# Adjacency loads paced by the projection loop, adj @ x spread into the mixing, and sums scattered to natural order

## The chip, the cores and the metric

The kernel runs on one core of one Trainium2 chip. The metric is device microseconds (us) of one execution; a lower number is better. A profile is one execution, so its span can lie a few us from the median.

Engine names in profile lines: PE is TensorE (PEld its weight loads), DVE is VectorE, ACT is ScalarE, POOL is GpSimd, SP is SyncE, which here only issues transfers. L540 is line 540 of that kernel's own file; the same statement has another line number in another kernel.

## The reference

Four graph layers act on `x` of 8 x 2048 x 64, each followed by a residual and a layer norm. The change touches only the first layer and the way its result is handed on.

```python
# layer 0: hypergraph attention
h = x @ W                                               # the loop over h
s = leaky_relu(h @ a_node, 0.2)
alpha = softmax(where(H.T > 0, s, NEG)); agg = alpha @ h
beta = sigmoid((h @ a_gn)[:, None] + (agg @ a_ge)[..., None])
all_he = elu(beta * h + (1 - beta) * agg)
se = attn_scores(elu(agg))                              # tanh(f @ fcW + fcb) @ av
g = sum_e softmax(where(H > 0, se, NEG)) * all_he       # the slot loop
industry = (adj / deg) @ (x @ W_ind)                    # adj @ x, "filler" matmuls
out = weighted_pair(industry, g)                        # the mixing
x = layernorm(x + out)
# layer 1
x = layernorm(x + (dinv * (adj + I) * dinv) @ x @ W.T)
# layers 2 and 3: unchanged by this edit
```

A node belongs to few hyperedges, so `g` is computed by slots: nodes are sorted by how many hyperedges they have, 128 nodes to a tile, and tile t needs only as many slots as its fullest node. There are 57 slots in 16 tiles. `adj` is 2048 x 2048 float32, held as 16 tiles of 1 MB.

## The kernel before

Its first 640 us run in stages on all engines. The loop over h has 16 steps; it projects `x`, stores the rows `hs` in HBM for later gathering, and accumulates the hyperedge sums `pagg`. The table chain turns `pagg` into small tables, while the first filler matmuls (`du`, row sums of `adj`) run in between. `fill(n)` issues the next n matmuls of adj @ x; there are 64 of `du` and 512 of `ug`, about 0.23 us each.

```python
XT = NT // 8; XB = XT * NP                       # 8 x buffers; 14 adjacency tiles issued at once
for t in range(NT - XT):
    if t in (0, 1):
        tc.keep_in_program_order(nc.gpsimd.tensor_copy(seen_x, xt[2 * t + 1][:, 0, 0:1]))
    load_adj(t)                                  # 1 MB, from GpSimd's queue
# ...
for t in range(NT):                              # the loop over h
    # ph = xt[t] @ bd66 (4 matmuls)
    fetch_xt(t + XB)
    st = pa.tile([P, HROW], F32, tag="st", name="st", bufs=4)
    # seen, exponentials, st, ex on DVE and ACT
    nc.scalar.dma_start(hs_hbm[t * P:(t + 1) * P, :], st)
    # pagg += m_n.T @ ex
# ... table chain with fill(24), fill(14), fill(14), fill(12)
```

A one-hot is a matrix of zeros with a single 1 for each node; multiplied with a table it picks, for every node of a tile, the row of the node's hyperedge in that slot. `pz` is that row plus the node's own row, `ps` the same for the few columns of scores, from which the factors `R` and `co` are made. In the slot loop each slot has three `pz` matmuls, nine filler matmuls, three DVE operations, one exponential and one GpSimd sum:

```python
for t in range(NT):
    S, both, ohs, R, co = now                    # begin(t): gathered rows, hi/lo split, ps, coefficients
    for s in range(S):
        # pz = rows + one_hot[s] @ table (3 matmuls)
        if s == 0 and t + 1 < NT:
            fill(3)
            now = begin(t + 1)
        fill(9)
        if s == max(0, S - 5) and t + 2 < NT:
            slots(t + 2, pps, "mm", 3)           # GpSimd makes the one-hots of tile t + 2
        nc.vector.tensor_tensor(z, z, R[:, s, :, None].to_broadcast([P, B, F]), ALU.mult)
        y = pl.tile([P, B, F], F32, tag="y", name="y", bufs=2)
        nc.scalar.activation(y, z, AF.Exp, bias=-1.0)
        nc.vector.scalar_tensor_tensor(y, z, 1.0, y, op0=ALU.max, op1=ALU.min)
        # y * co on DVE; acc + y on GpSimd (not for s == 0)
    nc.sync.dma_start(gs_hbm[t * P:(t + 1) * P, :], acc.rearrange("p b f -> p (b f)"))   # sorted order
for _ in filler:
    pass
```

The mixing has 16 steps; each gathers its rows of `g` back to natural order. From the sixth step on, layer 1's matmuls are the filler (10 in each of four places a step). Layer 1 leaves three of its four results in SBUF; the third goes through HBM.

```python
    for j in range(JT):                          # mix_parts(i): 4 indirect gathers a step
        nc.gpsimd.indirect_dma_start(out=gn[:, j, :], in_=g_rows, in_offset=IndirectOffsetOnAxis(rank4[...]), ...)
# ...
for i in range(steps + 1):
    k = 10 if i > NCH else 0                     # no filler in the first five steps
    # mix_parts, fill(k), mix_weigh, fill(k), mix_scores, fill(k), mix_end, fill(k)
fill(40)
nc.scalar.dma_start(xn[2], x2_hbm[:])
```

## Time and profile before

The median was 2234.11 us in 3 runs (2231.68 to 2234.51).

| stage (profile of before) | from, to (us) | length | what fills it |
|---|---|---|---|
| loop over h | 21.0, 80.4 | 59.4 | DMA until 60 us, then steps of 1.85 us |
| table chain | 80.4, 110.1 | 29.7 | filler, waits for GpSimd |
| slot loop | 110.1, 288.5 | 178.4 | PE 94% busy |
| mixing alone | 288.5, 347.0 | 58.5 | PE 41.5 busy |
| mixing and layer 1 | 347.0, 639.6 | 292.6 | PE 82% busy |
| layers 2 and 3 | 639.6, 2233.5 | 1593.9 | not changed |

### The profile page before, as it was taken

How to read it: one execution, taken by the hardware profiler on the slowest of the kernel's cores; microseconds unless marked ns; L12 is line 12 of the kernel's file. 1: busy time of each engine (PE TensorE's matmuls, PEld its weight loads, DVE VectorE, ACT ScalarE, POOL GpSimd, SP SyncE). 2: the span in 40 equal slices, each digit the busy share in tenths (PEclk: the TensorE clock that was granted, in tenths of full speed). 3: DMA queues.
4: the chain of work that ended last, by engine and by line, in shares of the span. 5: the costliest groups of instructions: out<-in, count | busy, mean ns of one | idle time of the engine just before them, and what ended most of it. 6: DMA issues, size and time to landing. Idle time of an engine off the chain costs nothing. (4 is left out here: it accounts for less than half of the span.)

```text
span 2233.5 us, 19741 instructions
## 1 busy us (share of the span) xinstructions
PE 1979.0 (89%) x7292; PEld 1279.6 (57%) x7292; DVE 1115.8 (50%) x1833; ACT 374.7 (17%) x688; POOL 553.8 (25%) x507
## 2 busy tenths in 40 slices
PE   4899969888749999799999999999896999999994
PEld 3578725555634444474465456456444777777773
DVE  4478846666532222217845864772883233333322
ACT  1223333232111111010010010001001112222110
POOL 2377866564222322100100010110110010110102
PEclk7899979999869999899999999999998999999997
DMA  9412333222210000100000000000001112111110
GB/s 368 162 54 93 106 103 95 90 66 71 81 16 0 19 19 19 43 1 7 7 5 5 7 8 3 7 10 0 10 5 41 38 27 55 37 52 38 48 29 21
DMA packets 65706, 104.31 MB, mean 47 GB/s; under 512 B 27312, under 2 KB 27344, under 8 KB 63360
## 3 DMA queue, kind: packets, MB, share of 16 engines
q1 hardware_dynamic: 54432, 70.51, 10.4%
q0 software_dynamic: 5856, 25.89, 3.5%
q10 hardware_dynamic: 5312, 6.56, 0.9%
q8 instruction: 59, 0.97, 0.2%
q14 instruction: 47, 0.39, 0.1%
HBM read 76.13 MB, written 26.80 MB: 46 GB/s over the span
## 5 line engine op out<-in xcount | busy, mean ns | idle before, releaser
L1020 PE MATMUL py<-wp,xg 128*128 128x512 f32 x1024 | 448.6, 597 | 8.5 <-DVE fcav L1025 5.8
L1020 PEld LDWEIGHTS py<-wp,xg 128*128 128x128 f32 x1024 | 193.6, 191 | 254.4 <-issue 216.2
L177 PE MATMUL u<-adj,hi 128*128 128x512 f32 x768 | 258.0, 417 | 0.0
L177 PE MATMUL u<-adj,lo 128*128 128x512 f32 x768 | 249.0, 404 | 0.0
L967 PE MATMUL u<-pt,xn 128*128 128x512 f32 x512 | 230.5, 609 | 8.3 <-DVE u L976 7.1
L1025 DVE TENSOR_TENSOR fcav<-py,emb_n 128x512 f32<-128x512 f32 x256 | 177.1, 692 | 52.1 <-PE py L1020 37.2
L1028 POOL TENSOR_TENSOR r<-r,bias 128x256 f32<-128x256 f32 x32 | 23.3, 729 | 636.2 <-DVE r L1026 636.2
L1026 DVE TENSOR_REDUCE r<-fcav 128x32 f32<-128x512 f32 x256 | 175.4, 685 | 8.1
L967 PEld LDWEIGHTS u<-pt,xn 128*128 128x128 f32 x512 | 98.5, 195 | 132.0 <-issue 117.0
L645 PE MATMUL u<-adj,vh 128*128 128x512 f32 x512 | 158.8, 409 | 14.7 <-ACT vh L168 10.9
L177 PEld LDWEIGHTS u<-adj,hi 128*128 128x128 f32 x768 | 144.3, 192 | 41.2 <-issue 11.2
L177 PEld LDWEIGHTS u<-adj,lo 128*128 128x128 f32 x768 | 146.1, 192 | 34.3
L645 PE MATMUL u<-adj,vl 128*128 128x512 f32 x512 | 152.1, 399 | 0.0
L156 POOL TENSOR_TENSOR ln_r<-ln_e,neg_half 128x8 f32<-128x8 f32 x64 | 106.1, 1659 | 169.3 <-DVE ln_e L154 167.9
L961 DVE TENSOR_SCALAR pt<-pt 128x512 f32<-128x512 f32 x64 | 48.8, 781 | 175.4 <-ACT pt L960 174.0
L1116 DVE SCALAR_TENSOR_TENSOR fcav<-fcav,ar 128x512 f32<-128x512 f32 x64 | 44.3, 693 | 176.4 <-ACT ar L1115 176.3
L1098 POOL TENSOR_TENSOR r<-r,xn 128x512 f32<-128x512 f32 x16 | 20.4, 1278 | 435.0 <-DVE r L1097 435.0
L645 PEld LDWEIGHTS u<-adj,vh 128*128 128x128 f32 x512 | 96.4, 190 | 45.1 <-ACT vh L168 12.4
L965 POOL TENSOR_TENSOR acc<-acc,pt 128x512 f32<-128x512 f32 x60 | 79.6, 1327 | 165.9 <-DVE pt L961 163.1
L645 PEld LDWEIGHTS u<-adj,vl 128*128 128x128 f32 x512 | 96.6, 189 | 22.2 <-issue 0.7
L150 ACT ACTIVATE r<-ln_c 128x512 f32<-128x512 f32 x64 | 40.4, 631 | 264.7 <-DVE ln_c L146 253.3
L762 POOL DMA_INDIRECT gn<-gs_hbm,rank x64 | 69.7, 1089 | 34.2 <-PE pg L180 14.6
(339 smaller groups left out, 2748.5 us busy)
## 6 DMA issues: line engine op xcount, KB each, us to landing
adj<-in_adj_t POOLq DMA_DIRECT2D x16, 1024.0 KB
fcav<-in_adj_t SPq DMA_DIRECT2D x64, 256.0 KB
x_hbm<-r SPq DMA_DIRECT2D x20, 256.0 KB
hs_hbm<-st ACTq DMA_DIRECT2D x16, 292.0 KB
xt<-in_x_t SPq DMA_DIRECT2D x16, 256.0 KB
xc<-in_x_n SPq DMA_DIRECT2D x16, 256.0 KB
u_hbm<-ut SPq DMA_DIRECT2D x16, 256.0 KB
gs_hbm<-acc SPq DMA_DIRECT2D x16, 256.0 KB
```

Source lines behind the costliest of these rows:

```text
L150: nc.scalar.activation(r, xc, AF.Square)
L156: nc.gpsimd.tensor_tensor(rstd, vare, neg_half[:, :groups], ALU.pow)
L177: tc.keep_in_program_order(nc.tensor.matmul(*args, **kw))
L645: nc.tensor.matmul(u[c], lhsT=half[:, j, :], rhs=adj[t][:, cols(c)], start=t == 0 and i == 0, stop=ends and not own,)
L762: nc.gpsimd.indirect_dma_start(out=gn[:, j, :], out_offset=None, in_=g_rows, in_offset=bass.IndirectOffsetOnAxis(ap=rank4[:, p, c * JT + j ...
L961: nc.vector.tensor_scalar(pt, pt, 1.0, None, op0=ALU.max)
L965: nc.gpsimd.tensor_tensor(acc, acc, pt, ALU.add)
L967: nc.tensor.matmul(u[p], lhsT=xn[p][:, t, :], rhs=pt, start=t == 0, stop=t == NT - 1)
L1020: nc.tensor.matmul(py.rearrange("p o d -> p (o d)"), lhsT=xg[b][:, q, cols(j, P)], rhs=wp[:, q, cols(k)], start=q == 0, stop=q == 1,)
L1025: nc.vector.tensor_tensor(pr, py, e_b, ALU.mult)
L1026: nc.vector.tensor_reduce(r[:, j, b, cols(k, OH)], pr, AX.X, ALU.add)
L1116: nc.vector.scalar_tensor_tensor(a, a, 1.0, ar.bitcast(F32), op0=ALU.mult, op1=ALU.not_equal, accum_out=left[:, t, k:k + 1],)
```

## The change

Four ideas belong together. The adjacency loads no longer go out at once but after certain steps of the loop over h, so that the row writes need not queue behind them. Filler leaves the slot loop (9 to 6 a slot) for the mixing's first five steps, where TensorE was idle. The sums of the slot loop are scattered to natural order, so that 64 gathers of the mixing become 16 plain loads. The pools are laid out anew for this: fewer x buffers, `x` chunks fetched in the loop, and all of layer 1's results but the last through HBM. The diff, cut to its core:

```diff
-    XT = NT // 8
-    XB = XT * NP
+    XT, XB = 1, NP
@@ adjacency
-        for t in range(NT - XT):
-            if t in (0, 1):
-                tc.keep_in_program_order(nc.gpsimd.tensor_copy(seen_x, xt[2 * t + 1][:, 0, 0:1]))
+        def load_adj_after(t, what):
+            tc.keep_in_program_order(nc.gpsimd.tensor_copy(seen_x, what))
             load_adj(t)
+        for t in range(5):
+            load_adj_after(t, xt[min(t, 3)][:, 0, 0:1])
+        paced = {1: 5, 2: 6, 4: 7, 5: 8, 7: 9, 8: 10, 10: 11, 11: 12, 13: 13, 14: 14}
@@ loop over h
+            if t in paced:
+                load_adj_after(paced[t], seen[:, t, 0, 0:1])
+            if t in (NT // 2, NT // 2 + 2):
+                c = (t - NT // 2) // 2
+                fetch(0, c)
+                parts(0, c)
@@ one-hots
-            made = nc.gpsimd.tensor_scalar(o, slot, float(s + 1), None, op0=ALU.is_equal)
+            eng = nc.vector if t == 0 and s % 3 < 2 else nc.gpsimd
+            made = eng.tensor_scalar(o, slot, float(s + 1), None, op0=ALU.is_equal)
@@ table chain: fills 24 + 14 + 14 + 12 become 24 + 14 + 10 + 24, tile 0's one-hots come after them in program order
@@ slot loop
-                fill(9)
+                fill(6)
-            nc.sync.dma_start(gs_hbm[t * P:(t + 1) * P, :], acc.rearrange("p b f -> p (b f)"))
-        for _ in filler:
-            pass
+            nc.gpsimd.indirect_dma_start(
+                out=gs_hbm[:], out_offset=bass.IndirectOffsetOnAxis(ap=order[:, t:t + 1], axis=0),
+                in_=acc.rearrange("p b f -> p (b f)"), in_offset=None,
+            )
@@ mixing
-        for j in range(JT):
-            nc.gpsimd.indirect_dma_start(
-                out=gn[:, j, :], out_offset=None, in_=g_rows,
-                in_offset=bass.IndirectOffsetOnAxis(ap=rank4[:, p, c * JT + j:c * JT + j + 1], axis=0),
-            )
+        nc.sync.dma_start(
+            gn, gs_hbm[c * C:(c + 1) * C, p * P:(p + 1) * P].rearrange("(t p) f -> p t f", p=P)
+        )
-        k = 10 if i > NCH else 0
+        k = 10 if i > NCH else 8
@@ layer 1's results
-        if p != 2:
+        if p == NP - 1:
             layernorm(lp, grouped(r), grouped(xn[p][:, wide(c), :]))
         else:
             layernorm(lp, grouped(r), grouped(r))
-            nc.sync.dma_start(x2_hbm[:, wide(c), :], r)
+            nc.sync.dma_start(x2_hbm[p][:, wide(c), :], r)
@@ after the mixing
+    for p in range(2):
+        nc.scalar.dma_start(xn[p], x2_hbm[p][:])
     fill(40)
-    nc.scalar.dma_start(xn[2], x2_hbm[:])
+    nc.scalar.dma_start(xn[2], x2_hbm[2][:])
```

More of the change, by code (lines that the diff above doesn't have):

```diff
@@ L166, in split @@
         lo = pool.tile(shape, F32R, tag=f"{tag}l", name=f"{tag}l", bufs=bufs)
-        steps = (
-            nc.scalar.copy(hi, src),
-            eng.tensor_tensor(lo, src, hi.bitcast(F32) if eng is nc.gpsimd else hi, ALU.subtract),
-        )
-        if pin:
-            for i in steps:
-                tc.keep_in_program_order(i)
+        kept = tc.keep_in_program_order if pin else lambda i: i
+        kept(nc.scalar.copy(hi, src))
+        kept(eng.tensor_tensor(lo, src, hi.bitcast(F32) if eng is nc.gpsimd else hi, ALU.subtract))
         return hi, lo
@@ L198, in tile_gnn_fast @@
     av_col = const.tile([P, 1], F32, name="av_col")
-    rank4 = const.tile([P, NP, NT], U32, name="rank4")
     wrong = const.tile([P, 6], F32, name="wrong")
     nc.vector.memset(wrong, 0.0)
+    va_scope = ExitStack()
+    va = va_scope.enter_context(tc.tile_pool(name="va", bufs=1))
     hy_scope = ExitStack()
@@ L209, in staged @@
     def staged(name):
-        return hy.tile([P, JT, P], F32, tag="x", name=name, bufs=2)
+        return va.tile([P, JT, P], F32, tag="x", name=name, bufs=2)
     def load_adj(t):
@@ L222, in tile_gnn_fast @@
     x1_hbm = [dram.tile([P, NT, P], F32, name=f"x1_hbm{p}") for p in range(NP)]
-    x2_hbm = dram.tile([P, NT, P], F32, name="x2_hbm")
+    x2_hbm = [dram.tile([P, NT, P], F32, name=f"x2_hbm{p}") for p in range(NP - 1)]
     gs_hbm = dram.tile([N, BF], F32, name="gs_hbm")
@@ L253, in slots @@
         for s in range(sum(n > t for n in SLOT_TILES)):
-            o = hy.tile([P, P], F32R, tag="o", name="o", bufs=17)
-            made = nc.gpsimd.tensor_scalar(o, slot, float(s + 1), None, op0=ALU.is_equal)
+            o = hrp.tile([P, P], F32R, tag="o", name="o", bufs=17)
+            eng = nc.vector if t == 0 and s % 3 < 2 else nc.gpsimd
+            made = eng.tensor_scalar(o, slot, float(s + 1), None, op0=ALU.is_equal)
             if t == 0:
@@ L264, in tile_gnn_fast, with fetch, parts @@
     places = {}
-    def products():
-        xc = {}
-        def fetch(p, c):
-            xc[p, c] = staged("xc")
-            load_x(xc[p, c], p, c)
-        part = {}
-        def parts(p, c):
-            part[c] = split(hy, xc.pop((p, c)), f"v{c}", 1, [P, JT, P], nc.gpsimd)
-        for c in range(NCH):
-            fetch(0, c)
-            parts(0, c)
+    xc, part = {}, {}
+    def fetch(p, c):
+        xc[p, c] = staged("xc")
+        load_x(xc[p, c], p, c)
+    def parts(p, c):
+        part[c] = split(va, xc.pop((p, c)), f"v{c}", 1, [P, JT, P], nc.gpsimd, p == 0)
+    def products():
         du = [pph.tile([P, 2, C], F32, tag="ph", name=f"du{g}", bufs=2) for g in range(2)]
@@ L328, in products @@
                             transpose(pt[:, cols(j, P)], deg1[:, k:k + 1].to_broadcast([P, P]))
-                        inv.append(places["sbuf"](f"inv{c}"))
+                        inv.append(va.tile([P, C], F32, name=f"inv{c}"))
                         nc.scalar.copy(inv[c], pt)
                 for c in own:
-                    ut = places["ut"]()
+                    ut = va.tile([P, C], F32, tag="ut", name="ut", bufs=2)
                     nc.vector.tensor_tensor(ut, u[c], inv[c], ALU.mult)
@@ L344, in tile_gnn_fast @@
     pph = ph_scope.enter_context(tc.tile_pool(name="ph", bufs=1, space=PSUM))
-    with tc.tile_pool(name="pa", bufs=1) as pa, tc.tile_pool(name="pa_ps", bufs=1, space=PSUM) as pps:
+    with tc.tile_pool(name="pa_ps", bufs=1, space=PSUM) as pps:
+        pa_scope = ExitStack()
+        pa = pa_scope.enter_context(tc.tile_pool(name="pa", bufs=1))
         xs_scope = ExitStack()
@@ L386, in tile_gnn_fast @@
         nc.gpsimd.memset(avz, 0.0)
-        age = pa.tile([P, F], F32, name="age")
+        age = hy.tile([P, F], F32, name="age")
         nc.gpsimd.dma_start(age, bass.AP(tensor=a_ge.tensor, offset=a_ge.offset, ap=[[0, P], [1, F]]))
@@ L445, in tile_gnn_fast @@
         nc.vector.tensor_reduce(rank, gt, AX.X, ALU.add)
-        for p in range(NP):
-            nc.vector.tensor_scalar(rank4[:, p, :], rank, float(NP), float(p), op0=ALU.mult, op1=ALU.add)
         over = so.tile([P, BINS], F32, name="over")
@@ L504, in tile_gnn_fast @@
         so_scope.close()
-        ta_scope = ExitStack()
         seen = pa.tile([P, NT, B, 2], F32, name="seen")
@@ L533, in tile_gnn_fast @@
             )
-            nc.scalar.activation(ex[:, :, :, F], lr.rearrange("p (k g) -> p k g", k=2), AF.Exp)
+            tc.keep_in_program_order(
+                nc.scalar.activation(ex[:, :, :, F], lr.rearrange("p (k g) -> p k g", k=2), AF.Exp)
+            )
             for k in range(2):
@@ L555, in tile_gnn_fast @@
         adj += [adj_end.tile([P, N], F32R, name=f"adj{t}") for t in range(NT - XT, NT)]
+        load_adj(NT - 1)
         fetch_rows(0)
         fetch_rows(1)
-        for t in range(NT - XT, NT):
-            load_adj(t)
-        ta = ta_scope.enter_context(tc.tile_pool(name="ta", bufs=1))
+        for c in (2, 3):
+            fetch(0, c)
+            parts(0, c)
+        pa_scope.close()
+        hrp_scope = ExitStack()
+        hrp = hrp_scope.enter_context(tc.tile_pool(name="hrp", bufs=1))
+        ta_scope = ExitStack()
+        ta = ta_scope.enter_context(tc.tile_pool(name="ta", bufs=1, side="right"))
         ones_r = ta.tile([P, P], F32R, name="ones_r")
@@ L574, in tile_gnn_fast @@
         nc.vector.reciprocal(den, den)
-        agg = pa.tile([P, G, F], F32, tag="ex", name="agg", bufs=2)
+        agg = ta.tile([P, G, F], F32, name="agg")
         nc.vector.tensor_tensor(agg, gv[:, :, 0:F], den[:, :, None].to_broadcast([P, G, F]), ALU.mult)
-        he = pa.tile([P, G, F], F32, tag="ex", name="he", bufs=2)
+        he = ta.tile([P, G, F], F32, name="he")
         nc.scalar.activation(he, agg, AF.Exp)
@@ L592, in tile_gnn_fast @@
             nc.scalar.activation(tf[:, b], pf, AF.Tanh, bias=fcb_col)
-        fill(14)
-        tab = pa.tile([P, G, F], F32, tag="st", name="tab", bufs=4)
+        fill(10)
+        tab = ta.tile([P, G, F], F32, name="tab")
         tsm = ta.tile([P, 2, G], F32, name="tsm")
@@ L616, in tile_gnn_fast @@
         stack(tab2.rearrange("p (k n) -> p k n", k=2), tab.rearrange("p g f -> p (g f)"), "tabr", False)
-        slots(0, pps, "sm", 2)
-        fill(12)
         pse = pps.tile([P, 2, 2], F32, tag="sm", name="pse", bufs=2)
@@ L631, in tile_gnn_fast @@
         stack(ts2.rearrange("p (i k g) -> p k i g", i=2, k=2), tsm, "tsr", True)
+        slots(0, pps, "sm", 2)
+        fill(NT * NCH - 48 + 8)
         ta_scope.close()
@@ L658, in tile_gnn_fast @@
     with ExitStack() as pb_scope:
-        pb = pb_scope.enter_context(tc.tile_pool(name="pb", bufs=1, side="right"))
         pps = pb_scope.enter_context(tc.tile_pool(name="pb_ps", bufs=1, space=PSUM))
         places["small"] = lambda shape, name: pps.tile(shape, F32, tag="mm", name=name, bufs=3)
-        places["ut"] = lambda: pb.tile([P, C], F32, tag="ut", name="ut", bufs=2)
-        places["sbuf"] = lambda name: pb.tile([P, C], F32, name=name)
         pl = pb_scope.enter_context(tc.tile_pool(name="pl", bufs=1))
@@ L670, in begin @@
             hrow = hrows.pop(t)
-            both = split(hy, hrow[:, 0:BF], "hr", 2, [P, BF], nc.vector if t == 0 else nc.gpsimd, t == 0)
+            both = split(hrp, hrow[:, 0:BF], "hr", 2, [P, BF], nc.vector if t == 0 else nc.gpsimd, t == 0)
             ohs = one_hot.pop(t)
@@ L716, in tile_gnn_fast @@
                     nc.gpsimd.tensor_tensor(acc, acc, y, ALU.add)
-            nc.sync.dma_start(gs_hbm[t * P:(t + 1) * P, :], acc.rearrange("p b f -> p (b f)"))
-        for _ in filler:
-            pass
-    ph_scope.close()
+            nc.gpsimd.indirect_dma_start(
+                out=gs_hbm[:], out_offset=bass.IndirectOffsetOnAxis(ap=order[:, t:t + 1], axis=0),
+                in_=acc.rearrange("p b f -> p (b f)"), in_offset=None,
+            )
+    hrp_scope.close()
     hy_scope.close()
@@ L737, in tick @@
             pending.pop(0)[1]()
-    xn = [None] * NP
-    xn01 = ctx.enter_context(tc.tile_pool(name="xn01", bufs=1))
-    for p in range(2):
-        xn[p] = xn01.tile([P, NT, P], F32, name=f"xn{p}")
-    l1_scope = ExitStack()
-    lp = l1_scope.enter_context(tc.tile_pool(name="l1", bufs=1))
-    lps = l1_scope.enter_context(tc.tile_pool(name="l1_ps", bufs=1, space=PSUM))
     mix_scope = ExitStack()
-    mp = mix_scope.enter_context(tc.tile_pool(name="mix", bufs=1))
-    bd_w1 = on_diagonal(lp, w1_t, "bd_w1")
-    g_rows = gs_hbm[:].rearrange("n (p f) -> (n p) f", f=P)
+    mp = mix_scope.enter_context(tc.tile_pool(name="mix", bufs=1, side="right"))
+    lps_scope = ExitStack()
+    lps = lps_scope.enter_context(tc.tile_pool(name="l1_ps", bufs=1, space=PSUM))
     def wide(c):
@@ L760, in mix_parts @@
         gn = mp.tile([P, JT, P], F32, tag="gn", name="gn", bufs=2)
-        for j in range(JT):
-            nc.gpsimd.indirect_dma_start(
-                out=gn[:, j, :], out_offset=None, in_=g_rows,
-                in_offset=bass.IndirectOffsetOnAxis(ap=rank4[:, p, c * JT + j:c * JT + j + 1], axis=0),
-            )
+        nc.sync.dma_start(
+            gn, gs_hbm[c * C:(c + 1) * C, p * P:(p + 1) * P].rearrange("(t p) f -> p t f", p=P)
+        )
         ut = mp.tile([P, C], F32, tag="ut0", name="ut0", bufs=2)
@@ L804, in mix_end @@
         p, c = divmod(i, NCH)
-        r = lp.tile([P, JT, P], F32, tag="r", name="r", bufs=3)
+        r = mp.tile([P, JT, P], F32, tag="r", name="r", bufs=2)
         load_x(r, p, c)
@@ L810, in mix_end @@
         nc.vector.tensor_tensor(r, pt.rearrange("p (t f) -> p t f", f=P), r, ALU.add)
-        layernorm(lp, grouped(r), grouped(r))
+        layernorm(mp, grouped(r), grouped(r))
         nc.sync.dma_start(x1_hbm[p][:, wide(c), :], r)
-    part = [None] * NCH
     def l1_parts(p, c):
@@ L827, in l1_end @@
         nc.sync.dma_start(x1, x1_hbm[p][:, wide(c), :])
-        r = lp.tile([P, JT, P], F32, tag="r", name="r", bufs=3)
+        r = lp.tile([P, JT, P], F32, tag="r", name="r", bufs=2)
         nc.vector.tensor_tensor(r, po, dinv[:, wide(c), None].to_broadcast([P, JT, P]), ALU.mult)
         nc.gpsimd.tensor_tensor(r, r, x1, ALU.add)
-        if p != 2:
+        if p == NP - 1:
             layernorm(lp, grouped(r), grouped(xn[p][:, wide(c), :]))
@@ L840, in layer1 @@
             own = (2 * g, 2 * g + 1)
-            u = {c: lps.tile([P, C], F32, tag=f"u{c}", name=f"u{c}", bufs=1) for c in own}
+            ug = pph.tile([P, 2, C], F32, tag="ph", name="u1", bufs=2)
+            u = {c: ug[:, c % 2, :] for c in own}
             for t in range(NT):
@@ L871, in all_pairs @@
             yield from layer1(p)
-    filler = all_pairs()
-    def fill(n):
-        for _ in range(n):
-            next(filler, None)
     steps = NP * NCH
     for i in range(steps + 1):
-        k = 10 if i > NCH else 0
+        k = 10 if i > NCH else 8
         if i < steps:
@@ L894, in tile_gnn_fast @@
         if i == NCH:
+            for _ in filler:
+                pass
+            va_scope.close()
+            l1_scope = ExitStack()
+            lp = l1_scope.enter_context(tc.tile_pool(name="l1", bufs=1))
+            bd_w1 = on_diagonal(lp, w1_t, "bd_w1")
             for c in range(NCH):
                 l1_parts(0, c)
+            filler = all_pairs()
     mix_scope.close()
-    xn23 = ctx.enter_context(tc.tile_pool(name="xn23", bufs=1, side="right"))
-    for p in range(2, NP):
-        xn[p] = xn23.tile([P, NT, P], F32, name=f"xn{p}")
+    xnp = ctx.enter_context(tc.tile_pool(name="xnp", bufs=1, side="right"))
+    xn = [xnp.tile([P, NT, P], F32, name=f"xn{p}") for p in range(NP)]
+    for p in range(2):
+        nc.scalar.dma_start(xn[p], x2_hbm[p][:])
     fill(40)
-    nc.scalar.dma_start(xn[2], x2_hbm[:])
+    nc.scalar.dma_start(xn[2], x2_hbm[2][:])
     for _ in filler:
@@ L907, in tile_gnn_fast @@
     l1_scope.close()
+    lps_scope.close()
+    ph_scope.close()
     with tc.tile_pool(name="l2c", bufs=1) as cp:
```

## The prediction

> **What bounds the kernel now.** I read first the busy time by stretch. The stretches are cut where the trace shows a stage change: initial loads, loop over h, table chain, loop over slots (from its first DVE product to the last sum), mixing alone, mixing with layer 1, rest. Columns: PE, PEld, DVE, ACT, POOL busy, PE clock, DMA share, GB/s.
>
> ```profile
> 0.00:21.00 21.00, 3.66 (x36) 3.23 (x37) 6.98 (x23) 1.28 (x1) 12.48 (x50) 1.00 0.98 291
> 21.00:80.40 59.40, 42.80 (x210) 28.35 (x208) 33.23 (x118) 10.20 (x50) 2.65 (x5) 0.68 0.83 323
> 80.40:110.10 29.70, 23.24 (x98) 18.69 (x97) 10.13 (x23) 8.27 (x22) 16.61 (x23) 0.85 0.40 133
> 110.10:288.50 178.40, 167.69 (x759) 135.06 (x758) 144.25 (x251) 56.42 (x115) 132.84 (x126) 0.98 0.26 83
> 288.50:347.00 58.50, 41.50 (x107) 18.61 (x108) 27.79 (x38) 21.49 (x34) 44.38 (x40) 0.82 0.37 113
> 347.00:640.00 293.00, 240.03 (x1015) 168.87 (x1013) 176.61 (x259) 70.76 (x118) 143.85 (x106) 0.94 0.23 73
> ```
>
> The slot loop is TensorE's (94% busy, DVE 81%, POOL 74%). Mixing alone leaves TensorE 17 us idle and at a clock of 0.82. The change touches only these 640 us; the other 1593.5 us (layers 2 and 3) keep their code.
>
> Second, the timeline of ScalarE in the loop over h. Its copy into the row buffer `st` (four buffers) waits for earlier rows to land in HBM:
>
> ```profile
> 36.56 0.24 ACT L527 CAST st<-slot 128x64 f32<-128x64 bf16 x1 [4.67 <-DMA hs_hbm<-st]
> 45.41 0.24 ACT L527 CAST st<-slot 128x64 f32<-128x64 bf16 x1 [7.73 <-DMA hs_hbm<-st]
> 53.54 0.24 ACT L527 CAST st<-slot 128x64 f32<-128x64 bf16 x1 [5.51 <-DMA hs_hbm<-st]
> ...
> 71.10 0.23 ACT L527 CAST st<-slot 128x64 f32<-128x64 bf16 x1
> 73.04 0.23 ACT L527 CAST st<-slot 128x64 f32<-128x64 bf16 x1
> ```
>
> While adjacency is in flight, seven steps take 32 us; afterwards a step takes about 1.85 us.
>
> Third, VectorE's timeline in the slot loop, one slot of three operations:
>
> ```profile
> 171.12 0.68 DVE L706 TENSOR_TENSOR pz<-pz,R 128x512 f32<-128x512 f32 x1
> 172.52 0.69 DVE L710 SCALAR_TENSOR_TENSOR y<-pz,y 128x512 f32<-128x512 f32 x1 [0.72 <-ACT y L708]
> 173.25 0.69 DVE L715 TENSOR_TENSOR y<-y,co 128x512 f32<-128x512 f32 x1
> 173.86 0.69 DVE L706 TENSOR_TENSOR pz<-pz,R 128x512 f32<-128x512 f32 x1
> ```
>
> The period is 2.7 us, and 0.72 us of it DVE stands waiting for the exponential: in this order DVE alone would need as long as TensorE's twelve matmuls (12 x 0.23). The waits of layer 1's stretch (347 to 640) come fourth:
>
> ```profile
> PE pf L177 <- DVE ind L771: 12.7, 4, 4.5
> PE pt L180 <- DVE ind L801: 12.2, 4, 8.1
> ```
>
> **What the Trainium skill says.** "DMA: Bandwidth & Descriptors", section "Issuing engines are not separate DMA queues": transfers of all issuers share the same 16 engines and interleave. The trace agrees: `st` writes of ACT's queue are late by 3 to 8 us only while POOL's adjacency loads run. "TensorE: Matmul & The Clock Gate", Part 1: after idleness the array runs at half rate until it has been busy for a few us. It agrees: the eight matmuls of `ph` take 2.13 us at 43 to 53 us and 1.17 us after 67 us. "SBUF — State Buffer", "Who interferes with whom": a DVE instruction with two SBUF inputs contends with a GpSimd instruction that reads SBUF. It agrees: L715 (two SBUF inputs) has a mean of 933 ns against 689 ns for L710, which reads PSUM.
>
> **The change, part by part.**
>
> 1. *Loop over h, adjacency paced.* Loads 5 to 14 are issued after given steps. DMA then bounds the loop: by its end it must move m_n and m_en 1 MB, xt 4, st 4.7, x for two chunks 0.5, and about 12 to 13 MB of adjacency, together some 22.7 MB. The stretches above moved 6.1 MB in the first 21 us, and the saturated 25 to 50 us ran at 414 GB/s: (22.7 - 6.1) / 0.414 = 40 us, so the loop ends at 61, with some waits 63 instead of 80.4. **Gain 17.** (At 1.85 us a step it would end at 51, but the pacing itself ties it to the transfers.) The last three tiles land near 71, before the degree matmuls want them.
>
> 2. *Table chain.* Before, 80.4 to 110.1, with TensorE waiting 6.3 us for POOL's twelve one-hots (7.4 us). After, eight of twelve go to DVE and 24 fills stand ahead of their use. TensorE: 72 fills x 0.245 = 17.6, transposes and small products 3, `ps` 12 x 0.22 = 2.7, then 1.7 for the coefficients: 25 us against 29.7. **Gain 4.5**, with 8 more fills done.
>
> 3. *Slot loop.* 57 slots with 6 fills instead of 9. TensorE: 171 `pz` + 57 `ps` + 387 fills (57x6 + 15x3) + some 20 others = 635 x 0.225 = 143. The instruction order shows DVE's next product now mostly ahead of y*co, so the exponential is covered; its period is 0.6 + 0.69 + 0.75, about 2.1 us, and with 1 us a tile for coefficients and 8 of `ut` it needs about 148. POOL had 133; it gains 16 scatters. An indirect DMA costs it 1.09 plus 0.3 before the next (gather rows): +20, so 153. Taking the largest of the three tile by tile (tile 0: 28; two of five slots: 12.5 each; three of four: 11; four of three: 9; five of two: 6.5; the last 3) gives 157, and 160 with friction between queues. **Gain 18.** TensorE's 94% becomes about 88%, and POOL is the fullest.
>
> 4. *Mixing alone.* The gathers (4 a step, 1.25 us each) leave POOL for one plain transfer, but they were not what ended the steps for long: `pg` waited 2.8 us. In their place come 576 - 72 - 387 = 117 fills, 27 us of TensorE. At full clock a step has pi 0.9, pg 0.6, pf 3.4, pd 1.7, pt 0.5 = 7.2 us, plus 32 x 0.23 = 7.3. Tail: last scatter, its landing, gn's landing, about 7 us from the last sum (8 before). Then step 0 about 11, three steps of 14.7, the fifth 9, and the next inputs 1.5: 73 us against 58.5. **Loss 14.5.** So of the 27 us moved, 12 hide in idle time and in the lower clock.
>
> 5. *Mixing with layer 1 and its end.* 36 gathers leave POOL (41.8 busy). DVE waits 55 us for `ln_r` in 28 places, 1.96 each, where 1.8 is the power's own time; so only about 4 us was queueing behind gathers. The instruction order now puts work into that wait in 10 of the 28 instead of 3, worth 0.6 each, 4 us; two chunks more go through HBM, hidden. **Gain 7**, as TensorE's waits here are for DVE. The idle 20 us before layer 2 remain: its embeddings still wait for the last layer norm.
>
> Sum: 17 + 4.5 + 18 - 14.5 + 7 = 32. 2234 - 32 = **2202 us**, 1.4% less.
>
> **Rivals.**
> A. *The moved matmuls are mostly hidden and POOL does not bind.* For it: POOL spans are rough, 17 us of idle in mixing, and a clock that rises with steady work. Slot loop 150, mixing 66, loop over h to 58: 32 + 10 + 7 + 5 = 54, so 2180. Against it: fills and mixing share one in-order queue, and a step has as much fill as work.
> B. *POOL takes TensorE's place.* Scatters sit in front of sums and one-hots in POOL's order, and denser POOL work lengthens L715. Slot loop 170, mixing 75: gain 32 - 10 - 2 = 20, so 2214. For it: the late tiles of two slots have about 7 us of POOL against 6.2 us of TensorE before.
> C. *Pacing only delays adjacency.* If the loads fall behind, the degree matmuls wait at 80 us for tiles 12 to 15, and part 1 shrinks to 8: 2211. Against it: DMA is below 0.5 after 75 us now, so there is room.
>
> **Range and chances.** The parts are uncertain by about 5 (h), 8 (slot loop), 6 (mixing) and 6 (layer 1): together 13 us as independent terms. I give 2184 to 2222 for eight in ten. Over 2% needs under about 2190, which A reaches: 0.22. Slower by over 2% would need a loss of 45 us in stages that only lose terms: 0.02. The rest, 0.76, is within 2%.
>
> **What would show it.** Right: `st` waits almost gone and the last `pagg` near 63; the first `pz` product near 88; the last slot sum near 248, with POOL busiest; the first layer-1 matmul near 321, PE clock near 1 in mixing; end of layer 1's layer norm near 607. Wrong: an h loop that still ends after 72 (C); a slot loop under 152 (A) or over 168 (B); mixing alone under 66, meaning the fills hid; or layer 1 moving by over 15 either way, which would mean that the new DVE order, which I only counted, decides. A change of over 5 us in layers 2 and 3 would break the premise that they keep their time.

## The result, and the profile after

The changed kernel took 2244.02 us in the median of 4 runs (2239.38 to 2246.92) beside 2234.31 of the kernel before. The ratio is 1.0042, 95% interval 1.0020 to 1.0064: slower by 0.4%. A ratio is the mean time of one kernel's runs over the mean of the other's in the same rounds, so it is not quite the ratio of the medians quoted. Where an experiment is set against the changed kernel below, its ratio to before is divided by 1.0042 or the medians are subtracted; such a difference is good to some 5 us.

| event (us in the profile) | before | predicted | after |
|---|---|---|---|
| last `pagg` (end of loop over h) | 80.4 | 63 | 79.9 |
| first slot product | 110.1 | 88 | 103.9 |
| end of slot loop | 288.5 | 248 | 284.8 |
| first layer-1 matmul | 347.0 | 321 | 362.0 |
| last layer-1 layer norm | 639.6 | 607 | 651.1 |
| end of layers 2 and 3 | 2233.5 | | 2240.4 |

The same view as the first of the prediction, busy time by stretch, now of the changed kernel: loop over h, table chain, slot loop, mixing alone, mixing with layer 1.

```profile
21.00:79.90 58.90, 43.01 (x213) 28.33 (x210) 32.75 (x114) 10.95 (x51) 10.15 (x23) 0.76 0.94 335
79.90:103.90 24.00, 23.09 (x106) 18.53 (x106) 9.26 (x32) 7.75 (x21) 9.95 (x12) 0.95 0.42 146
103.90:284.80 180.90, 151.34 (x632) 116.47 (x631) 143.17 (x247) 56.45 (x115) 147.25 (x139) 0.95 0.23 75
284.80:362.00 77.20, 63.63 (x226) 40.54 (x226) 35.09 (x48) 22.84 (x35) 19.95 (x15) 0.90 0.32 103
362.00:651.10 289.10, 241.01 (x1012) 171.46 (x1012) 166.91 (x255) 70.55 (x117) 101.08 (x67) 0.93 0.26 88
```

By length: 58.9 us for 59.4, 24.0 for 29.7, 180.9 for 178.4, 77.2 for 58.5, 289.1 for 292.6. Layers 2 and 3 take 1589.3 for 1593.9, of which I make nothing. So the loop over h gained nothing. The slot loop shed 127 matmuls of TensorE (759 to 632) and became no shorter: TensorE went from 168 to 151 us busy, and GpSimd from 133 to 147. The mixing took what was moved into it.

**The loop over h.** ScalarE's timeline of the changed kernel, the same copies into the row buffer that the prediction showed:

```profile
33.23 0.24 ACT L520 CAST st<-slot 128x64 f32<-128x64 bf16 x1 [7.52 <-DMA hs_hbm<-st]
...
50.54 0.24 ACT L520 CAST st<-slot 128x64 f32<-128x64 bf16 x1 [5.95 <-DMA hs_hbm<-st]
...
69.28 0.24 ACT L520 CAST st<-slot 128x64 f32<-128x64 bf16 x1 [3.86 <-DMA hs_hbm<-st]
...
74.84 0.24 ACT L520 CAST st<-slot 128x64 f32<-128x64 bf16 x1 [2.94 <-DMA hs_hbm<-st]
```

The copies still wait for rows to land, but at the end of the loop too: the paced loads now collide with the last steps. One profile places the end of this loop only to some 3 us: in the ten profiles with this order of loads it lies between 76.6 and 82.3 us.

**The slot loop.** GpSimd's timeline for a tile of three slots in the changed kernel (start, duration, engine, line, operation; idle before it in brackets):

```profile
172.87 1.28 POOL L719 TENSOR_TENSOR acc<-acc,y 128x512 f32<-128x512 f32 x1 [0.69 <-DVE R L685]
174.11 0.97 POOL L252 TENSOR_SCALAR o<-slot 128x128 fp32r<-128x128 bf16 x1
175.25 1.06 POOL L721 DMA_INDIRECT gs_hbm<-acc,order  x1 [0.17 <-POOL o L252]
176.61 1.00 POOL L234 DMA_INDIRECT hrow<-hs_hbm,order  x1 [0.30 <-issue]
177.64 1.68 POOL L252 TENSOR_SCALAR o<-slot 128x128 fp32r<-128x128 bf16 x3
179.96 1.74 POOL L169 TENSOR_TENSOR hrl<-hrow,hrh 128x512 fp32r<-128x512 f32 x1 [0.64 <-ACT hrh L168]
```

GpSimd goes from a sum to a one-hot, the scatter (L721), the next gather of rows (L234), three one-hots, a split and the next sums with hardly a break. Its two indirect transfers cost 1.06 and 1.00 us, with 0.17 and 0.30 us of idle time before them. "GPSIMD Engine Reference", section 4.1 "Engine selection", in the Trainium skill says that GpSimd is about twice as slow as VectorE for an operation with two inputs; this trace agrees (1.29 us the median of its 128x512 sum, 0.68 to 0.69 us for VectorE's 128x512 product where nothing disturbs it). The waits of the slot loop in the changed kernel (who waited, for whom: us in total, times, longest):

```profile
ACT y L711 <- POOL acc L719: 41.7, 17, 6.0
...
PEld ps L173 <- POOL o L252: 13.6, 15, 2.9
...
PE ps L173 <- POOL o L252: 10.4, 14, 2.7
```

In the kernel before, the first of these was 6.7 us and the other two together 0.7. The last two are waits of TensorE for the one-hots, by its weight loads and by its matmuls; most are the same stops seen twice, so they are not to be added (an expectation below does add them, to 24 us). Where GpSimd is not in the way, the change works as meant: the first six sums of tile 0 came 2.0 us apart, where a slot took 2.7 before.

**The end of layer 1.** ScalarE's timeline of the changed kernel, then TensorE's:

```profile
587.28 0.83 ACTq L896 DMA_DIRECT2D xn<-x_hbm  x2
593.27 0.62 ACT L168 CAST v3h<-y 128x512 fp32r<-128x512 f32 x1 [7.52 <-DMA xn<-x_hbm]
...
614.40 0.33 ACTq L898 DMA_DIRECT2D xn<-x_hbm  x1
614.83 0.59 ACT L858 COPY ut<-u 128x512 f32<-128x512 f32 x1 [6.05 <-DMA x_hbm<-r]
```

```profile
615.47 2.08 PE L173 MATMUL po<-bd_w,ut 128*128 128x128 f32 x8 [4.87 <-ACT ut L858]
```

Two things could be at work around the reloads of `xn`. The first two, 1 MB each, go out at 587 us beside layer 1's own loads of 256 KB. ScalarE's split of layer 1's input `y` then starts after 7.52 us of idle time (the view names the reload, but the split needs `y`, and VectorE's scaling of `y` had waited 4.59 us for one of the small loads), and GpSimd's next sum waits 13.15 us for an input:

```profile
597.48 1.28 POOL L823 TENSOR_TENSOR r<-r,x 128x512 f32<-128x512 f32 x1 [13.15 <-DMA x<-x_hbm]
```

The third stands in ScalarE's queue until the layer norms that it reads have been written; ScalarE stands idle for 6.05 us before a copy of a result behind it, and for that copy TensorE stops for 4.87 us. "Perfetto Trace Analysis", section "Tensor Engine Instruction (MATMUL, LD_WEIGHTS)", in the Trainium skill says that the execution queues of ScalarE, VectorE and GpSimd are strictly first in, first out; the copy that waits behind a transfer fits that, though the passage speaks of the engines' instructions and not of transfers. This third reload is not new: the kernel before has it, with the same wait in ScalarE's timeline, so only the first two can be a cost of the change.

```profile
603.42 0.58 ACT L864 COPY ut<-u 128x512 f32<-128x512 f32 x1 [6.16 <-DMA x_hbm<-r]
```

### The profile page after: what moved, and what is told of

Its sections match the earlier page's. It is cut to its first block, busy times and chain, and to the rows that moved or that the text cites. A ratio compares the mean times of both kernels' runs of the same rounds, so it can differ in the third digit from the quotient of the medians.

```text
span 2240.4 us, 19695 instructions
## 1 busy us (share of the span) xinstructions
PE 1981.7 (88%) x7292; PEld 1282.5 (57%) x7292; DVE 1110.8 (50%) x1837; ACT 376.2 (17%) x688; POOL 501.0 (22%) x464
## 5 line engine op out<-in xcount | busy, mean ns | idle before, releaser
L652 PEld LDWEIGHTS u<-adj,vh 128*128 128x128 f32 x512 | 96.4, 190 | 45.5 <-ACT vh L168 12.5
L144 DVE TENSOR_REDUCE ln_m<-r 128x8 f32<-128x512 f32 x64 | 43.8, 685 | 70.0 <-POOL r L1030 27.9
```

Of the source, the lines that this page charges most:

```text
L144: nc.vector.tensor_reduce(mean, r, AX.X, ALU.add)
L652: nc.tensor.matmul(u[c], lhsT=half[:, j, :], rhs=adj[t][:, cols(c)], start=t == 0 and i == 0, stop=ends and not own,)
```

## The experiments

All have the changed kernel as base. Fourteen kernels ran, in four batches; the kernel before was at 2234.4, 2234.3, 2231.2 and 2235.2 us in the four.

### 1. The scatter undone

```diff
-            nc.gpsimd.indirect_dma_start(out=gs_hbm[:], out_offset=...order[:, t:t + 1]..., in_=acc...)
+            nc.sync.dma_start(gs_hbm[t * P:(t + 1) * P, :], acc.rearrange("p b f -> p (b f)"))
@@ mix_parts: the four indirect gathers a step, and rank4, are back
```

> The changed kernel with the sums written in sorted order by a plain transfer again and gathered, four rows sets a step, in the mixing; all else as changed. Theory (GpSimd binds the changed slot loop: busy 147 of 181 us, and 0.3 us dead after each indirect transfer): 16 scatters of about 1.05 + 0.3 us leave it, the slot loop falls from 181 to about 160 us, the gathers fit into GpSimd's idle time in the mixing, total about 2222 (2214 to 2230). Rival (the order of VectorE's products and sums binds, or TensorE's in-order queue): slot loop stays at 175 to 181, total 2238 or more.

Measured: 2242.99 us (2236.71 to 2245.87, 6 runs), ratio to before 1.0041: no change against the changed kernel. Yet its slot loop is shorter by 13 us:

```profile
99.80:267.60 167.80, 147.67 (x632) 114.57 (x631) 146.31 (x247) 56.50 (x115) 133.83 (x125) 0.97 0.26 80
267.60:346.20 78.60, 65.82 (x225) 40.70 (x225) 35.62 (x48) 22.71 (x35) 47.52 (x43) 0.89 0.36 104
346.20:642.20 296.00, 243.63 (x1012) 171.06 (x1012) 170.40 (x255) 70.33 (x117) 140.29 (x102) 0.92 0.27 85
```

So the theory holds for the slot loop (167.8 us for 180.9, most of the way to 160) and fails for the total. The profile gives back 1.4 us in the mixing and 7 in layer 1, where GpSimd is 140 us busy instead of 101; it also fell on the fastest of the six runs. The scatter is a real cost where it was put (13.1 us) and a real gain where it came from (8.3 us), and the two largely cancel. (The loop over h and the table chain, which the edit leaves alone, were 4.1 us shorter in this profile; layers 2 and 3 were 3.4 longer.) What happens to the rest, about 6 us between profile and median, this run does not tell.

### 2. Eight filler matmuls after a slot

```diff
-                fill(6)
+                fill(8)
```

> The changed kernel with 8 adjacency matmuls after a slot in place of 6, so that only 3 are left for the mixing alone. Theory (GpSimd binds the slot loop and leaves TensorE 30 us idle there): the 114 more matmuls (26 us of TensorE) fill that idle time, slot loop 183 to 187, mixing alone 77 down to about 54, total about 2222 (2215 to 2230). Rival (the slot loop's length is set by TensorE's queue, stalls and all): slot loop about 205, mixing alone 54, total unchanged at 2238 to 2246.

Measured: 2220.68 us (2216.09 to 2229.74, 6 runs), ratio 0.9940 [0.9918, 0.9962]: 23 us under the changed kernel.

```profile
105.10:293.80 188.70, 172.09 (x746) 135.42 (x745) 151.51 (x249) 56.51 (x115) 150.17 (x140) 0.97 0.23 74
293.80:349.20 55.40, 40.25 (x112) 19.17 (x112) 29.62 (x41) 21.27 (x34) 18.43 (x13) 0.88 0.40 124
```

TensorE took 114 more matmuls in the slot loop for 7.8 us more (188.7), and the mixing alone became 21.8 us shorter. The rival had 205. The 26 us of filler cost 7.8 us where it was taken from and 21.8 where it was put. The kernel before did 13 more matmuls in a slot loop of 178.4 us: with nearly the same filler the new slot loop is 10.3 us longer.

### 3. Adjacency after the loop

```diff
-        paced = {1: 5, 2: 6, 4: 7, 5: 8, 7: 9, 8: 10, 10: 11, 11: 12, 13: 13, 14: 14}
+        paced = {}
-        load_adj(NT - 1)
+        for t in range(5, NT):
+            load_adj(t)
```

> The changed kernel with adjacency tiles 5 to 14 loaded after the loop over h and not paced within it. Theory (the loop is bound by the bytes that must pass in it, some 19.7 MB at 335 GB/s of which 10 are adjacency): without them its steps take 1.85 us, the last aggregate matmul comes near 55 instead of 79.9 us, the degree matmuls then wait for tiles, the first slot product comes near 85 to 90 instead of 103.9, total about 2224 (2218 to 2232). Rival (something else than the DMA engines' bytes holds the loop, such as the latency of the row writes): the loop still ends after 72, the degree matmuls wait on top, total 2240 to 2255.

Measured: 2245.19 us (2240.78 to 2246.58, 6 runs), ratio 1.0045. Neither expectation holds whole. The stretches are the loop and the chain; the wait is from the chain:

```profile
21.00:67.40 46.40, 36.79 (x214) 23.88 (x211) 32.83 (x114) 11.68 (x52) 7.26 (x11) 0.86 0.76 257
67.40:106.30 38.90, 26.30 (x107) 20.36 (x106) 9.18 (x31) 7.22 (x20) 10.98 (x14) 0.77 0.76 292
```

```profile
PEld pslot L176 <- DMA hrow<-hs_hbm,order: 10.2, 1, 10.2
```

The loop ends 12.5 us earlier, the chain takes 14.9 longer: the first gather of rows waits behind the adjacency, and the first slot product comes at 106.3 (103.9). (GpSimd issued the loads from 56 us on, after its splits in program order, and not at the loop's end, so they overlapped its last five steps.) Two things follow. The adjacency loads do hold the loop. And it could not have ended at 55 without them: its first three steps are interleaved with the sorting of rows and end near 39 us; thirteen steps of 1.85 us after that make 63, an estimate from these numbers.

### 4. The reloads of layer 1's results moved to the end

```diff
-    for p in range(2):
-        nc.scalar.dma_start(xn[p], x2_hbm[p][:])
-    fill(40)
-    nc.scalar.dma_start(xn[2], x2_hbm[2][:])
     for _ in filler:
         pass
     while pending:
         tick()
+    for p in range(NP - 1):
+        nc.sync.dma_start(xn[p], x2_hbm[p][:])
```

> The changed kernel with the three reloads of layer 1's results moved behind layer 1's last work and onto SyncE's queue; nothing else. Theory (waiting transfers at the head of ScalarE's queue stop its copies, 7.5 and 6.05 us, TensorE idles 3.8 and 4.9 us and runs at half clock after): layer 1's last layer norm ends near 640 instead of 651 and total is about 2230 (2226 to 2234). Rival (the same wait only moves, as the loads of 3 MB then stand between layer 1 and layer 2): total 2238 to 2246.

Measured: 2226.66 us (2224.01 to 2229.81, 6 runs), ratio 0.9965 [0.9950, 0.9979]: 17 us under the changed kernel.

```profile
359.30:634.00 274.70, 234.51 (x1012) 167.71 (x1012) 170.25 (x255) 70.39 (x117) 101.40 (x67) 0.95 0.28 92
```

Mixing with layer 1 takes 274.7 us for 289.1, with the same work; layers 2 and 3 take 2 us more (1591.6 for 1589.3). The rival falls. But the scheduler did not leave the loads at the end: the trace has them on SyncE's queue at 584.6, 591.1 and 603.3 us, each when its data was there. So this run took away the blocked queue and also spread the bytes, and my theory named only the first. Two more kernels part them.

### 4a and 4b. The first two reloads alone, the third alone

```diff
-    for p in range(2):                                             # 4a
-        nc.scalar.dma_start(xn[p], x2_hbm[p][:])
     fill(40)
     nc.scalar.dma_start(xn[2], x2_hbm[2][:])
@@ after layer 1's last work
+    for p in range(2):
+        tc.keep_in_program_order(nc.scalar.dma_start(xn[p], x2_hbm[p][:]))
```

```diff
-    nc.scalar.dma_start(xn[2], x2_hbm[2][:])                       # 4b
+    nc.sync.dma_start(xn[2], x2_hbm[2][:])
```

> The changed kernel with only the first two reloads of 1 MB each held back on ScalarE's queue until its last layer norm; the third stays where it was. The trace of the changed kernel shows both at 587 us, next to layer 1's own loads of 256 KB, which then land 9.2 us after their issue instead of 2.5, so that GpSimd waits 13.2 us for one. Theory A (their bytes crowd layer 1's own loads out): these waits go, total about 2234 (2230 to 2237), the wait of 6 us before the third reload stays. Theory B (only the waiting transfer at the head of ScalarE's queue costs): total within 4 us of the changed kernel's 2244.

> The changed kernel with only the third reload moved from ScalarE's to SyncE's queue, at the same place. Theory B (the waiting transfer at the head of ScalarE's queue, 6.05 us before a copy and 4.87 of TensorE): total about 2236 (2232 to 2239). Theory A (the bytes of the first two reloads do it all): total within 4 us of 2244. If both hold, each of the two kernels takes part of the 17 us that moving all three gained.

Measured: 4a 2234.24 us (2230.97 to 2235.91, 6 runs), ratio 0.9997 [0.9983, 1.0010], 10 us under the changed kernel; 4b 2229.64 us (2227.57 to 2233.84, 6 runs), ratio 0.9983 [0.9968, 0.9998], 13 under. GpSimd's sum and ScalarE's copy, first of 4a, then of 4b:

```profile
590.37 1.29 POOL L823 TENSOR_TENSOR r<-r,x 128x512 f32<-128x512 f32 x1 [6.68 <-DVE y L812]
```

```profile
607.39 0.59 ACT L858 COPY ut<-u 128x512 f32<-128x512 f32 x1 [6.15 <-DMA x_hbm<-r]
```

```profile
590.91 1.30 POOL L823 TENSOR_TENSOR r<-r,x 128x512 f32<-128x512 f32 x1 [13.23 <-DMA x<-x_hbm]
```

```profile
602.74 0.59 ACT L858 COPY ut<-u 128x512 f32<-128x512 f32 x1 [0.52 <-PE u L173]
```

Each edit removes its own wait and leaves the other's: 4a frees the sum from its load and keeps the blocked copy (6.15 us), 4b keeps the late load (13.23 us) and frees the copy (0.52). Mixing with layer 1 takes 281.7 and 280.5 us, 7.4 and 8.6 less than in the changed kernel; both at once took 14.4. So both causes are real and about equal; but the blocked copy stood in the kernel before as well, and only the crowding came with the change. (The 9.2 us in the expectation of 4a is SyncE's own wait for a load, not a time from issue to landing.)

### 5 and 6. Which property of GpSimd binds the slot loop

One-hots of tiles 1 to 15 on ScalarE, exact for small integers:

```diff
-            made = eng.tensor_scalar(o, slot, float(s + 1), None, op0=ALU.is_equal)     # t > 0
+            nc.scalar.activation(sq, slot, AF.Square, bias=shift[:, s:s + 1])           # shift = -(s + 1)
+            nc.scalar.activation(o, sq, AF.Relu, scale=-1.0, bias=1.0)
```

> The changed kernel with the 45 one-hots of tiles 1 to 15 made by ScalarE (a square and a rectifier each, exact for small integers) in place of GpSimd; scatter kept. Theory (GpSimd binds the slot loop, first through one-hots that stand behind its sums and scatters, for which TensorE waits 24 us): 28 us of GpSimd's 147 go, those waits go, slot loop 181 to about 165, total about 2228 (2222 to 2236). Rival (what holds is the coupling of VectorE, ScalarE and GpSimd through the two buffers of y, not the amount of GpSimd work; ScalarE's copies now stand in the exponentials' way): slot loop 176 to 185, total 2238 to 2250.

Four buffers for `y`:

```diff
-                y = pl.tile([P, B, F], F32, tag="y", name="y", bufs=2)
+                y = pl.tile([P, B, F], F32, tag="y", name="y", bufs=4)
```

> The changed kernel with four buffers for y in place of two; nothing else. ScalarE's exponential waits 41.7 us for GpSimd to have added the y of two slots before. Rival of the theory that GpSimd's amount of work binds (coupling through y): exponentials run ahead, slot loop 181 to about 165, total about 2228. Theory (amount of work, GpSimd 147 us busy and 9 dead of 181): the wait moves to another buffer (the one-hots, the product's PSUM), slot loop 174 to 181, total 2237 to 2245.

Measured: one-hots on ScalarE 2227.28 us (2222.69 to 2230.45, 6 runs), ratio 0.9967 [0.9951, 0.9983]; four buffers 2239.40 us (2228.92 to 2247.34, 6 runs), ratio 1.0032 [1.0015, 1.0050]. The slot loop of each, in this order:

```profile
103.40:269.90 166.50, 143.88 (x632) 111.96 (x631) 148.05 (x247) 78.04 (x203) 120.66 (x96) 0.98 0.26 81
```

```profile
101.70:278.90 177.20, 151.22 (x632) 117.49 (x631) 148.43 (x247) 57.74 (x115) 147.62 (x139) 0.94 0.24 76
```

Taking 27 us of work off GpSimd shortens the loop by 14.4 us. Letting the exponentials run ahead gains nothing that can be resolved: the window above ends with VectorE's last sum, GpSimd's came at 280.1 us, which makes 178.4, and the eight profiles that leave the slot loop as it is have 178.5 to 180.7 by that measure. The wait moves as the theory said; in the waits of the kernel with four buffers:

```profile
PEld ps L173 <- POOL o L252: 15.0, 17, 3.0
...
ACT y L711 <- POOL acc L719: 5.4, 5, 1.9
```

ScalarE no longer waits for sums (5.4 us for 41.7), TensorE waits for the one-hots as before. So it is the amount of GpSimd's work, and within it the one-hots behind the sums and scatters. With experiment 1 this is shown twice.

### 7. Six row buffers in the loop over h

```diff
-            st = pa.tile([P, HROW], F32, tag="st", name="st", bufs=4)
+            st = pa.tile([P, HROW], F32, tag="st", name="st", bufs=6)
```

> The changed kernel with six row buffers in the loop over h in place of four (more do not fit); nothing else. ScalarE waits 29.9 us for row writes to land. Theory (the loop is bound by its bytes at what the DMA engines move): the waits move to the next-needed buffer, the last aggregate matmul comes at 76 to 80 instead of 79.9, total within 3 us of the changed kernel's 2244. Rival (latency of a row write with only four in flight binds): the loop ends near 68 to 72, total about 2234.

Measured: 2250.10 us (2244.71 to 2252.84, 6 runs), ratio 1.0068. The loop ended at 80.6 us, so the rival falls: more row writes in flight do not help. The 6 us lost come after it: in the new layout the constant of the degree matmuls lies where a row buffer was, and TensorE waits 9.6 us for that row to be written.

### 8 and 9. Other pacing

Tiles 5, 6 and 7 issued at the start and seven paced, and no pacing at all:

```diff
-        for t in range(5):
+        for t in range(8):
             load_adj_after(t, xt[min(t, 3)][:, 0, 0:1])
-        paced = {1: 5, 2: 6, 4: 7, 5: 8, 7: 9, 8: 10, 10: 11, 11: 12, 13: 13, 14: 14}
+        paced = {4: 8, 5: 9, 7: 10, 8: 11, 10: 12, 12: 13, 13: 14}
```

> The changed kernel with adjacency tiles 5, 6 and 7 issued with the first five, and the other seven paced by steps 4 to 13 (one to two steps later each). In the changed kernel DMA moved 278 GB/s from 25 to 50 us, where the first three steps are held by the sorting of rows and the pacing follows the steps, and 367 to 405 after. Theory (the loop's end is when its 19.7 MB have passed; the pacing let DMA idle for some 8 us of transfers): the gap is filled, the loop ends near 72 instead of 79.9, total about 2237 (2233 to 2241). Rival (only the order of transfers counts, the early tiles delay the first row writes and inputs): the loop ends at 78 to 82, total 2242 to 2248.

```diff
-        paced = {1: 5, 2: 6, 4: 7, 5: 8, 7: 9, 8: 10, 10: 11, 11: 12, 13: 13, 14: 14}
+        paced = {}
+        for t in range(5, NT - 1):
+            load_adj(t)
```

> The changed kernel with all fifteen adjacency tiles issued at once, as before the change; everything else as changed. This undoes the pacing alone. Theory (bytes decide, in whatever order): the loop ends within 3 us of the changed kernel's 79.9, row writes wait early instead of late, total 2240 to 2248. Rival (the pacing gained and something else lost it): the loop ends after 85, total over 2250.

Measured: earlier pacing 2240.64 us (2235.83 to 2242.91, 6 runs), ratio 1.0027 [1.0008, 1.0045]; none 2237.54 us (2233.29 to 2243.60, 6 runs), ratio 1.0029 [1.0011, 1.0048]. Both intervals overlap that of the changed kernel. The loop ended at 82.2 and at 79.1 us, the first slot product came at 106.8 and 103.0. My theory for the first failed: filling the gap of 25 to 35 us (now over 400 GB/s) opened another at 35 to 45 (200 GB/s), as the next loads again wait for steps. The second kept the loop's end within 3 us, as expected, but not for the reason given: from 65 to 80 us it moved only 184 to 238 GB/s, so its last steps ran at their own speed after the loads had held up the first. Loads ahead of the steps or among them, the loop ended at about the same time; the pacing is worth nothing that these runs can resolve.

### 10 to 12. The gains together

Experiment 2 with 4; the two with 5; the three with the earlier pacing of 8. The edits are those shown.

> The changed kernel with both edits that gained: 8 adjacency matmuls after a slot, and layer 1's results reloaded behind its last work. The two lie in different stages, so they should add: 2244 - 23 - 17 = 2204 (2199 to 2211), 1.3% under the kernel before. If they share a cause (for instance the clock that is granted), less: 2212 or more.

> The three edits that gained, together: 8 matmuls after a slot, late reloads, one-hots of tiles 1 to 15 on ScalarE. In the slot loop the first and the third compete for the same idle time of TensorE: with 8 matmuls TensorE is busy 172 of 189 us, so the one-hots can win at most some 12 us there. Expected: slot loop about 181, total 2203 (2197 to 2210). If GpSimd no longer matters once TensorE is full: slot loop 187 to 190, total 2208 to 2213.

> The same three edits and the earlier pacing. If the pacing's gain of about 7 us holds and adds: total about 2196 (2190 to 2204). If the earlier pacing gains nothing: the same as the kernel with three edits, within 4 us.

| kernel | us, median (range, runs) | ratio to before, 95% interval |
|---|---|---|
| fill 8, late reloads | 2210.78 (2207.76 to 2211.82, 4) | 0.9897 [0.9880, 0.9914] |
| and one-hots on ScalarE | 2199.34 (2197.86 to 2201.35, 5) | 0.9850 [0.9831, 0.9869] |
| and earlier pacing | 2197.57 (2191.09 to 2203.07, 5) | 0.9837 [0.9814, 0.9860] |

The first two gains add but for some 7 us; the second row's slot loop is 174.8 us with TensorE 166 us busy, shorter than I expected (181). The third row's earlier pacing again gains nothing that can be resolved. The kernel with three edits beats both: 1.5% under the kernel before.

## Why the prediction was wrong

It named 2202 us with 2184 to 2222 as range; 2244 lies outside. By its own steps:

1. **Loop over h, gain 17: got 0.5.** Two terms of its one division failed. It had 16.6 MB still to move after 21 us; 58.9 us at 335 GB/s are 19.7. GpSimd's queue, which carries the adjacency, had moved 15.4 MB by the end of the loop (3.6 before 21 us, 11.8 after), where I had 12 to 13. It had the bytes at 414 GB/s throughout; pacing by steps that are themselves held by the sorting until 39 us left DMA at 188 to 295 GB/s between 25 and 45 us, and the mean was 335. At 414 GB/s, 19.7 MB would have passed at 68.6, so the bytes cost some 7.5 us and the rate 11. A remedy for the rate alone did not help (experiment 8), so this division describes what came and is no law. The remark that steps alone would end at 51 was wrong as well, as experiment 3 shows. Rival C, that pacing only delays adjacency, is what happened, though not at the degree matmuls where it expected the wait.
2. **Table chain, gain 4.5: got 5.7.** Right, and with the reason given: TensorE is 23.1 of 24.0 us busy. It holds without the pacing too (23.9 us in experiment 9).
3. **Slot loop, gain 18: lost 2.5.** This is the step that failed most. GpSimd's amount was foreseen (153 us predicted; 147 busy and 7 idle just before its indirect transfers). What failed is the rule "the largest of the three engines, tile by tile": in one tile GpSimd's sums, scatter, gather, one-hots and split are a queue, and the one-hots for which TensorE waits stand at its end. 181 us is what came, beyond even rival B's 170. Taking away the scatters gives 168, taking away the one-hots 166.5. Even without the scatters no engine is busy for more than 148 of these 168 us, so the rule fails there too; what fills the rest is not shown. Rival B's other sign came as well: VectorE's product of `y` with `co` took 1050 ns in the mean, 933 before.
4. **Mixing alone, loss 14.5: lost 18.7.** The mechanism was right, filler costs most of its time there (21.8 of 26 us in experiment 2). The tail is the mis-sized term: I gave 7 us from the last sum to the first input. It took 10.4, as the last scatter waits 2.5 us for the one before to land, and TensorE stood 15.9 us.
5. **Mixing with layer 1, gain 7: got 3.5.** The step that failed is "two chunks more go through HBM, hidden". Their reloads cost 7.4 us by crowding out layer 1's own loads (4a); without them the stage takes 281.7 us, a gain of 10.9 for the 7 predicted. About 7 of it came from the gathers (296.0 us with them in experiment 1, 289.1 without), where I gave 4; the rest would be VectorE's new order, which no run isolates. The blocked ScalarE costs about as much again (4b; both at once 14.4), but the kernel before had that wait too: taking it away is a gain beyond the change and not a loss that the change made.

Two small slips in the sums of step 3 did not matter: VectorE's terms add up to 144 us and not 148 (143 measured), and sixteen scatters at 1.39 us are 22 and not 20.

The sum of steps 1 to 5 was 32; 0.5 + 5.7 - 2.5 - 18.7 + 3.5 = -11.5, and layers 2 and 3 gave back 4.6 in the profile. The premise that they keep their time holds within the 5 us set for it. Open are the few us by which the profile of experiment 1 is faster than its median, and whether any order of loads can bring the first slot product well forward: the changed order gave 99.5 to 105.2 us in the ten profiles that have it (experiment 7 left out), the other orders 102.0 to 106.8.

## What to carry to other kernels

Filler moved off a stage gains only if the engine that had the filler sets the stage's length; look at what its neighbours need once it is gone, with the order of work in their own queues, and not at busy shares alone. A reload that nobody needs yet can still cost, by crowding out small loads that are needed now and by blocking the queue of the engine that issues it: moving three of them gained 17 us, and one of the three stood there before the change. Pacing transfers by steps that are themselves held up moves the wait without shortening it.

## What the Trainium skill lacked or had wrong

- "GPSIMD Engine Reference", section 4.1 "Engine selection": names GpSimd for gather and scatter and gives no cost on the issuing engine, and the page on DMA only a time to the first byte. Here a scatter of 128 rows occupied it for a median of 1.05 us, with up to 0.3 us of idle time just before most of them.
- "DMA: Bandwidth & Descriptors", section "Issuing engines are not separate DMA queues": agrees that transfers of all issuers interleave, but says nothing of small loads beside large ones. Here a load of 256 KB issued at 587.7 us beside two of 1 MB was waited for until 597.5, by GpSimd for 13.15 us in all; without the two, GpSimd waited 6.68 us for VectorE instead.
- No page says how to size a loop in which several engines are nearly full and hand work round: the fullest, TensorE, was busy 151 of 181 us here, and taking 27 us of work off GpSimd (147 us busy) shortened the loop by 14.4.
